# A fused four-stage kernel on one core: the setup ahead of the first softmax in another order

## The chip, the core and the metric

The kernel runs on one core of a Trainium2 chip. The metric is the device time of one execution in microseconds; the median of several executions counts. The data are float32 throughout, apart from the mask and a bfloat16 identity that is used to add it.

## What is computed

An input `x` of 16 items, 256 tokens by 256 features each, goes through four stages.

```python
# 0: adapter with an expert chosen per item, then a layer norm
h = gelu(x @ down_W.T + down_b) @ expert_W[id].T + expert_b[id] + domain_emb[id]
x = layernorm(h @ up_W.T + up_b + x) * gamma + beta
# 1: attention, scaled and shifted by an embedding of a timestep, then a feed-forward part
x = layernorm(x) * (1 + scale) + shift
s = q @ k.T / 4 + attention_bias          # 16 heads of 16; masked keys are -inf
x = x + softmax(s) @ v @ Wo + bo
x = x + gelu2(layernorm(x)*g2+beta2 @ W1 + b1) @ W2 + b2
# 2: one of three small networks, chosen per item, then a layer norm
# 3: finite differences of x on a 256 x 256 grid, one time step, max(., 0)
```

The attention bias alone is 16 x 16 x 256 x 256 floats (64 MB); it is read once, in pieces of four heads.

## The kernel before, in words

The items pass through the kernel as a stream. Nine generators each hold the work of one stage for all items: `adapt` (the adapter, two items at a time, called a pair), `prepare` (both norms ahead of the attention), `project` (q, k and v), `weigh` (scores and exponentials, four heads at a time), `attend` (transposing the weights and multiplying by v), `divide`, `enter` and `feed` (the rest of stage 1), `end` (stage 2) and `step` (stage 3). A planner, `Flow`, runs when the program is built. It keeps an estimated clock for each engine, which every generator advances with its costs (`flow.pe(1.0)`, `flow.dve(0.7, at)`), takes the generator that is due first among those that can start, and so fixes the order of the instructions on each engine. A `yield` gives the planner the choice: with a number it says when the next piece can start, with a function it says on what it depends (such as `("adapt", b) in done`). On the chip each engine then works through its own instructions in the order that the planner wrote down, and waits at each for its inputs.

What the change touches lies in the first 80 us. In the order of the program:

- Loads. SyncE asks for the tokens, `xt0` (the turned inputs of pair 0), the two expert matrices `e_w` of pair 0 (L303), `x0` (L251), the mask of item 0 (L378), the attention bias `side0` (L317), `x1`, `side1`, `Wo`, `side2`. ScalarE's queue asks for `w_down`, `cols`, `up`, `e_rows`, `w_ada` (L260), `rows_a` (L367) and `w_qkv` (L369), ahead of its first activation. All DMAs asked for by SyncE and ScalarE share eight semaphores, in turn; a DMA waits until the last one on its semaphore has landed.
- `idle` (L215) multiplies zeros; a count of 512 is one such matmul of 512 columns. It computes nothing that is used. Three run first (L226), one of 256 columns ahead of `p_u` (L570), and two ahead of pair 1 (L601).
- `adapt`, pair p: `p_h` (L543), a Gelu on ScalarE into `h1` (L547), `p_e` with the expert matrices (L558), `h2` on VectorE (L560; the trace calls `h1` and `h2` both `a_h`), `p_u` (L574), and the addition to each item's `x` on VectorE (L580). Beforehand `biased` (L527) has added the bias row `up_b` to `x` on GpSimd (L529). For pair 0 there are also `expert_bias`, `spread_mask(0)` (L382: the mask byte times a large negative number), `timestep` (Sin, Tanh, and the product `silu` on VectorE, L363), and `biased` for items 0 and 1.
- `prepare`, item b: statistics (L417 and L418 on VectorE, four small operations on GpSimd, L421 to L425: `rs` is one over the deviation), the first norm with gain and shift (L447 and L450 on VectorE for item 0; L456 and L457 on GpSimd for others), statistics again, and the second norm into `c_ln` (L433 or L438). For item 0 it also runs `condition` (`ps_a`, L500: 16-column matmuls that make scale and shift of all items) and, for item 1, `choose` (L970: 13 small operations on VectorE).
- `project`, item b: transposes `c_ln` (`c_t`, L464), scales it on ScalarE (`c_xt`, L632), multiplies by the three parts of `w_qkv` (`c_q` and `c_k` L646, `c_v` L689), and writes `c_qz` (L661 on VectorE, L665 on ScalarE), `c_kt` (L677) and `c_va` (L698).
- `weigh`, four heads m of item b: for item 0 it first adds the mask in the matmul (L733), then come the scores `c_s` (L738), and per head the bias and the row minimum on VectorE (L756) and the exponential on ScalarE (L767). For later items the mask is added to the bias by a DMA that GpSimd issues (L517).
- `attend` transposes the weights (`c_pt`), copies them out on VectorE (L472) or ScalarE (L474) and multiplies them by v (`c_c`, L821).

The Gelu, the Sin and the exponential need different function tables on ScalarE; the trace shows each change of table as an ACT_TABLE_LOAD.

Of the kernel before, what the change touches and what calls it, by code (L numbers as in the profile page):

```python
# [19 lines left out]
P = 128  # L20
B, S, D = 16, 256, 256
NC = S // P
# [148 lines left out]
def chain_kernel(ctx: ExitStack, tc: tile.TileContext, t: dict, out: bass.AP):  # L171
    nc = tc.nc
# [7 lines left out]
    def fixed(name, shape, dtype=F32, pool=const):  # L180
        return pool.tile(shape, dtype, name=name, tag=name)

    def load(name, src, shape, dtype=F32, engine=None, pool=const):
        got = fixed(name, shape, dtype, pool)
        (engine or nc.scalar).dma_start(out=got, in_=src)
        return got
# [4 lines left out]
    def chunked(w):  # L191
        return w.rearrange("(k p) n -> p k n", p=P)
# [3 lines left out]
    def misc(name, shape):  # L196
        numbers[name] = n = flow.take()
        return pp.tile(shape, F32, name=name, tag=f"m{n}")

    def free(name, at):  # L200

        flow.free_at[numbers.pop(name)] = at
        return at
# [11 lines left out]
    def idle(*columns):  # L215

        zeros = vas[1].rearrange("p c h e d -> p (c h e d)")
        name = f"idle{len(idles)}"
        idles.append(name)
        ps = misc(name, [P, NC * S])  # L220
        for n in columns:
            nc.tensor.matmul(ps[:, :n], zeros[:, :P], zeros[:, P : P + n], start=True, stop=True)
        free(name, flow.clock["PE"])
# [9 lines left out]
    def columns(name):  # L233
        return cols[:, COLUMN[name][0] : COLUMN[name][1]]
# [6 lines left out]
    def load_turned(p):  # L241

        arrives["t", p] = flow.clock["PE"] + 9.0 if p else 0.0
        xts[p] = xp.tile([P, 2, NC, S], F32, name=f"xt{p}", tag="xt", bufs=1)
        for i in range(2):
            nc.sync.dma_start(out=xts[p][:, i], in_=chunked(t["x_t"][2 * p + i]))

    def load_x(b):
        arrives["x", b] = flow.clock["PE"] + 7.0 if b > 1 else 0.0
        xs[b] = xp.tile([P, NC, D], F32, name=f"x{b}", tag="x", bufs=3)  # L250
        nc.sync.dma_start(out=xs[b], in_=chunked(t["x"][b]))  # L251
# [44 lines left out]
    e_ws = {}  # L296

    def load_expert(p):

        e_ws[p] = xp.tile([2 * A, A], F32, name=f"e_w{p}", tag="e_w")  # L300
        for i in range(2):
            e = nc.sync.value_load(e_idx[0:1, 2 * p + i : 2 * p + i + 1], min_val=0, max_val=E + 1)
            nc.sync.dma_start(  # L303
                out=e_ws[p][i * A : (i + 1) * A, :],
                in_=t["expert_W"][bass.ds(e, 1)].rearrange("e a o -> a (e o)"),
            )
# [51 lines left out]
    def timestep():  # L358
        for i, red in enumerate((sine, cosine)):
            nc.scalar.activation(emb[:, i, :], red, AF.Sin)  # L360
        nc.scalar.activation(th, emb, AF.Tanh, scale=0.5)
        nc.vector.tensor_scalar(emb, emb, 0.5, None, ALU.mult)
        nc.vector.scalar_tensor_tensor(silu, th, 1.0, emb, ALU.add, ALU.mult)  # L363
        flow.dve(0.25, flow.act(3.4))
# [1 line left out]

    rows_a = load("rows_a", rows(t["rows_a"]), [P, 5 * D])  # L367
    ln0_g, ln0_b, bv, bo, up_b = (rows_a[:, i * D : (i + 1) * D] for i in range(5))
    w_qkv = load("w_qkv", chunked(t["W_qkv"]), [P, NC, 3 * D])  # L369
    wq, wk, wv = (w_qkv[:, :, i * D : (i + 1) * D] for i in range(3))  # L370
    bqz = fixed("bqz", [P, NC])
    nc.vector.tensor_scalar(bqz, bq, columns("odd"), None, ALU.mult)
# [7 lines left out]
    def spread_mask(b):  # L380
        negs[b] = wp.tile([P, NC, S], BF16, name=f"neg{b}", tag="neg", bufs=2)
        nc.gpsimd.tensor_scalar(negs[b], m8s.pop(b), MASKED, None, ALU.mult)  # L382
        flow.pool(1.6)
# [96 lines left out]
    done = set()  # L480
    ready, ys, stats2, lns, hts, stats3 = {}, {}, {}, {}, {}, {}

    def expert_bias():

        ps_b = misc("ps_b", [2 * A, B // 2])
        for i in range(2):
            half = ps_b[i * A : (i + 1) * A, :]
            nc.tensor.matmul(half, e_rows[:, :A], e_hot[: E + 2, i::2], start=True, stop=False)
            nc.tensor.matmul(half, e_rows[:, A:], e_hot[: E + 2, i::2], start=False, stop=True)
        nc.vector.tensor_copy(e_add, ps_b)  # L490
        return free("ps_b", flow.dve(0.2, flow.pe(0.5)))
# [35 lines left out]
    def biased(b):  # L527
        x = xs[b]
        nc.gpsimd.tensor_tensor(x, x, up_b.unsqueeze(1).to_broadcast([P, NC, D]), ALU.add)  # L529
        flow.pool(1.35, arrives["x", b])  # L530
        done.add(("x", b))

    def adapt():

        for p in range(B // 2):
            yield lambda: p in e_ws
            yield arrives.get(("t", p), 0.0)
            parts = [slice(i * A, (i + 1) * A) for i in range(2)]
            w, xt = e_ws.pop(p), xts.pop(p)
            ps_h = misc(f"p_h{p}", [2 * A, S])  # L540
            for k in range(NC):
                for i in range(2):
                    nc.tensor.matmul(  # L543
                        ps_h[parts[i]], w_down[:, k, :], xt[:, i, k, :], start=k == 0, stop=k == NC - 1
                    )
            h1 = xp.tile([2 * A, S], F32, name=f"a_h1{p}", tag="a_h1", bufs=1)
            nc.scalar.activation(h1, ps_h, AF.Gelu, bias=columns("down_b"))  # L547
            at = free(f"p_h{p}", flow.act(0.47, flow.pe(1.0), "gelu"))
            if p == 0:
                expert_bias()  # L550
            yield at
            if p == 0:
                spread_mask(0)
                for b in range(2):
                    biased(b)
            ps_e = misc(f"p_e{p}", [2 * A, S])
            for i in range(2):
                nc.tensor.matmul(ps_e[parts[i]], w[parts[i]], h1[parts[i]], start=True, stop=True)  # L558
            h2 = xp.tile([2 * A, S], F32, name=f"a_h2{p}", tag="a_h2", bufs=1)
            nc.vector.tensor_scalar(h2, ps_e, e_add[:, p : p + 1], None, ALU.add)  # L560
            at = free(f"p_e{p}", flow.dve(0.4, flow.pe(0.5)))
            if p and 2 * p + 2 < B:
                load_turned(p + 1)
                load_expert(p + 1)
            if p:
                yield lambda: ("x", 2 * p + 1) in done
            yield at, 2
            if p == 0:
                timestep()
                idle(256)  # L570
            ps_u = [misc(f"p_u{2 * p + i}", [P, NC, D]) for i in range(2)]
            for c in range(NC):
                for i in range(2):
                    nc.tensor.matmul(  # L574
                        ps_u[i][:, c, :], h2[parts[i], c * P : (c + 1) * P], up[parts[i]], start=True, stop=True
                    )
            at = flow.pe(1.0)
            for b in (2 * p, 2 * p + 1):
                x = xs[b]
                nc.vector.tensor_tensor(x, ps_u[b % 2], x, ALU.add)  # L580
                adapted[b] = free(f"p_u{b}", flow.dve(0.7, at))
                done.add(("adapt", b))
                yield 0.0, 0

    def prepare():
        for b in range(B):
            yield lambda: ("adapt", b) in done
            x, at = xs.pop(b), adapted.pop(b)
            yield at, 0
            flow.spent += 0.75  # L590
            if b + 2 < B:
                load_x(b + 2)
                if b == 0:
                    load_turned(1)
                    load_expert(1)
            if b == 1:
                choose()
            stat, at = take_stats(f"0_{b}", x, at)
            if b == 0:
                condition()  # L600
                idle(512, 512)  # L601
            yield at, 0
            tmp = xp.tile([P, NC, D], F32, name=f"b_tmp{b}", tag="b_tmp", bufs=1)
            at = normalized_affine(x, x, stat, ln0_g, ln0_b, tmp, b == 0)
            yield at, 0
            stat, at = take_stats(f"1_{b}", x, at)
            if b == 0:
                conditioned()
                masked.update((m, 0.0) for m in range(4))
            yield at, 0  # L610
            if b > 1:
                yield lambda: ("turned", b - 2) in done
            ln = xp.tile([P, NC, D], F32, name=f"c_ln{b}", tag="c_ln", bufs=2)
            lns[b] = ln, normalized(ln, x, stat, b == 0)
            flow.spent += 1.5
            if b + 2 < B:
                biased(b + 2)
            done.add(("normal", b))

    def project():  # L620
# [622 lines left out]
```

## Time and profile before

| | us |
|---|---|
| median of three executions | 924.78 (921.94 to 926.36) |
| the profiled execution, its own time | 923.92 |
| its span, first to last instruction | 922.1 |
| TensorE matmuls busy | 882.4 (96%) |
| VectorE busy | 627.8 (68%) |
| ScalarE busy | 556.5 (60%) |
| GpSimd busy | 376.6 (41%) |
| mean granted TensorE clock | 0.978 |

The profile is of one execution. Its rows give for each instruction, or for a run of equal instructions, the start and the duration, and in brackets how long the engine had been idle before it and what ended that wait. PE is TensorE, PEld its weight loads, DVE is VectorE, ACT is ScalarE, POOL is GpSimd, SP is SyncE. A float32 matmul appears as two records. The granted clock is the share of full speed at which TensorE was allowed to run: a matmul of 256 columns takes about 380 ns at 1.00 and about 634 ns at 0.50 in this trace. The time of 922 us spans 40 slices on the page; TensorE's clock is 0.7 of full in the first of them, 0.6 in the second (both with rounding down to tenths) and 0.9 from the third to the last:

```profile
PE   7799898999999999999999999999999999999997
PEclk7699999999999999999999999999999999999999
DMA  9269978876777877778667776777667775850010
```

The DMA row is the busy share of the core's 16 DMA engines. They are full in the first slice, and again from about 65 to 112 us, when the large weights of the later stages are loaded beside the attention bias.

### The profile page before, as it was taken

Reading aid. Unit: us, or ns where it says so; the run is one execution under the profiler, and the core shown is the slowest. Engines: PE = TensorE matmul, PEld = TensorE weight load, DVE = VectorE, ACT = ScalarE, POOL = GpSimd, SP = SyncE. Lnnn points to the kernel's source line nnn. Section 1 sums busy time; section 2 is a strip of 40 time slices with the busy share of each in tenths; the row PEclk is TensorE's granted clock in tenths of the full one; section 3 lists DMA queues with packets and bytes.
Section 4 is the critical chain, followed back from the end, with each engine's and each line's share of the span. In section 5 each row is a group of like instructions: output and inputs, shape, how many; then the busy total and the mean of one; then the engine's idle time right before and its main releaser. Section 6 shows DMA issues by size and latency. Waiting matters only on the chain. (4 is left out here: it accounts for less than half of the span.)

```text
span 922.1 us, 18224 instructions
## 1 busy us (share of the span) xinstructions
PE 882.4 (96%) x6180; PEld 692.1 (75%) x6180; DVE 627.8 (68%) x2078; ACT 556.5 (60%) x1561; POOL 376.6 (41%) x514
## 2 busy tenths in 40 slices
PE   7799898999999999999999999999999999999997
PEld 4467585778787787877787778877878778877785
DVE  4477766888576777766767666766777676766443
ACT  2376747766566666766675767666675655656320
POOL 2234526653522425344543636154452525222331
PEclk7699999999999999999999999999999999999999
DMA  9269978876777877778667776777667775850010
GB/s 296 72 218 296 288 190 211 223 186 175 182 195 189 218 178 188 202 182 213 161 181 210 192 184 178 188 187 193 155 183 180 181 200 143 220 135 29 13 41 23
DMA packets 130972, 163.25 MB, mean 177 GB/s; under 512 B 12713, under 2 KB 94779, under 8 KB 130875
## 3 DMA queue, kind: packets, MB, share of 16 engines
q1 hardware_dynamic: 97920, 96.92, 33.1%
q0 software_dynamic: 31680, 62.92, 33.0%
q10 hardware_dynamic: 1275, 2.19, 0.7%
q8 instruction: 52, 0.85, 0.4%
q14 instruction: 45, 0.37, 0.1%
HBM read 94.89 MB, written 4.19 MB: 107 GB/s over the span
## 5 line engine op out<-in xcount | busy, mean ns | idle before, releaser
L767 ACT ACTIVATE c_pr<-c_sc,c_mx 128x256 f32<-128x256 f32 x512 | 254.9, 500 | 165.8 <-DVE c_mx L756 164.7
L756 DVE CUSTOM_DVE_ANT_0 c_sc<-c_s,side 128x256 f32<-128x256 f32 x512 | 193.6, 418 | 34.7 <-PE c_s L738 18.0
L464 PE MATMUL c_pt<-ident,c_pr 128*128 128x128 f32 x1024 | 143.5, 278 | 6.7 <-DVE x L580 2.1
L464 PEld LDWEIGHTS c_pt<-ident,c_pr 128*128 128x128 f32 x1024 | 116.8, 142 | 34.2 <-issue 11.9
L472 DVE COPY c_pts<-c_pt 128x512 f32<-128x512 f32 x175 | 117.2, 685 | 26.8 <-PE c_pt L464 26.5
L922 PE MATMUL d_f<-d_ht,w 128*128 128x256 f32 x512 | 122.3, 382 | 0.4
L421 POOL TENSOR_SCALAR rs<-mv 128x2 f32<-128x2 f32 x64 | 14.2, 222 | 253.2 <-DVE mv L418 252.7
L952 PE MATMUL d_o<-w,d_z 128*128 128x256 f32 x512 | 115.9, 380 | 0.1
L517 POOL DMA_DIRECT2D side<-neg x60 | 80.7, 1345 | 59.5 <-DMA side<-in_side 20.8
L952 PEld LDWEIGHTS d_o<-w,d_z 128*128 128x128 f32 x512 | 94.9, 190 | 12.5 <-DVE c_mx L756 0.6
L922 PEld LDWEIGHTS d_f<-d_ht,w 128*128 128x128 f32 x512 | 92.8, 190 | 15.1 <-issue 2.5
L767 ACT ACTIVATION_READ_ACCUMULATOR c_pr<-c_sc,c_mx 128x1 f32 x512 | 96.3, 188 | 0.0
L738 PE MATMUL c_s<-c_kt,c_qz 32*128 32x256 f32 x1024 | 78.3, 401 | 4.2 <-DVE c_mx L756 3.8
L821 PE MATMUL c_c<-c_pts,c_va 128*32 128x256 f32 x1024 | 72.6, 385 | 2.5 <-ACT c_pts L474 1.8
L738 PEld LDWEIGHTS c_s<-c_kt,c_qz 32*128 32x128 f32 x1024 | 49.1, 184 | 25.2 <-issue 12.2
L474 ACT COPY c_pts<-c_pt 128x512 f32<-128x512 f32 x81 | 45.5, 575 | 21.1 <-PE c_pt L464 21.0
L941 ACT ACTIVATE d_f<-d_z 128x512 f32<-128x512 f32 x64 | 38.4, 600 | 28.3 <-DVE d_z L938 27.2
L821 PEld LDWEIGHTS c_c<-c_pts,c_va 128*32 128x32 f32 x1024 | 27.9, 109 | 35.0 <-issue 18.2
L456 POOL TENSOR_TENSOR b_tmp<-b_tmp,rows_a 128x512 f32<-128x512 f32 x15 | 19.6, 1304 | 84.1 <-DVE b_tmp L433 65.7
L938 DVE TENSOR_SCALAR d_z<-d_f,cols 128x256 f32<-128x256 f32 x88 | 38.5, 479 | 17.3 <-PE d_f L922 17.2
L422 POOL TENSOR_TENSOR rs<-rs,inv_sqrt 128x2 f32<-128x2 f32 x64 | 46.0, 718 | 5.3
L960 DVE SCALAR_TENSOR_TENSOR y<-d_o,y 128x256 f32<-128x256 f32 x32 | 13.6, 424 | 45.4 <-PE d_o L952 45.4
(152 smaller groups left out, 1606.6 us busy)
## 6 DMA issues: line engine op xcount, KB each, us to landing
side<-in_side SPq DMA_DIRECT2D x256, 256.0 KB, 5.3
side<-neg POOLq DMA_DIRECT2D x60, 1024.0 KB, 8.1
d_w<-in_W_branch SPq DMA_DIRECT2D x16, 512.0 KB, 4.4
xt<-in_x_t SPq DMA_DIRECT2D x16, 256.0 KB, 5.2
x<-in_x SPq DMA_DIRECT2D x16, 256.0 KB, 5.9
out<-e_o SPq DMA_DIRECT2D x15, 256.0 KB, 3.9
w<-in_W SPq DMA_DIRECT2D x2, 1024.0 KB, 7.0
d_bout<-in_bl_branch SPq DMA_DIRECT2D x16, 128.0 KB, 4.3
```

Of the source, the lines that this page charges most:

```text
L422: nc.gpsimd.tensor_tensor(rs, rs, inv_sqrt, ALU.pow)
L464: nc.tensor.transpose(ps[:, k, c * P : (c + 1) * P], src[:, c, k * P : (k + 1) * P], ident)
L472: nc.vector.tensor_copy(dst, ps)
L474: nc.scalar.copy(dst, ps)
L517: nc.gpsimd.dma_start(out=sides[m].rearrange("p (h c) k -> p h (c k)", h=HB), in_=negs[m // 4].rearrange("p c k -> p (c k)").unsqueeze(1). ...
L738: nc.tensor.matmul(ps[i][:, c, :], qz[rows32, par, half, c * P : (c + 1) * P], k_t[rows32, half, :], start=b > 0, stop=b > 0 or c == NC - 1,)
L756: nc.vector.tensor_tensor_reduce(out=sc[:, c, :], in0=ps[i][:, c, :], in1=sb[:, i * NC + c, :], scale=-1.0, scalar=3.0e38, op0=ALU.add, op ...
L767: nc.scalar.activation(pr[:, c, :], sc[:, c, :], AF.Exp, bias=mx[:, c : c + 1], scale=-1.0, accum_out=sums[:, c, h : h + 1],)
L821: nc.tensor.matmul(ps_c[32 * i : 32 * i + 32, :], va[:, k, 4 * half + i, 2 * par : 2 * par + 2, :].rearrange("p e d -> p (e d)"), turned[i ...
L922: nc.tensor.matmul(ps_f[:, i, :], w1[:, k, f * P : (f + 1) * P], h_t[:, k, :], start=k == 0, stop=k == NC - 1,)
L938: nc.vector.tensor_scalar(z[:, i, :], ps_f[:, i, :], b1[:, f : f + 1], None, ALU.add)
L952: nc.tensor.matmul(ps_o, us[f // 2][:, f % 2, c * P : (c + 1) * P], w2[:, f, :], start=f == 0, stop=f == NF - 1,)
```

## The change

Five edits, all in the setup of the first items.

1. `W_qkv` is asked for on ScalarE's queue behind the first Gelu, instead of ahead of it.
2. In pair 0 the addition of `up_b` to item 0 is issued on GpSimd ahead of the spreading of item 0's mask, instead of behind it.
3. `up_b` is added to item 1 behind both norms of item 0 (together with that of item 2), instead of right after item 0's. Item 1's addition of the adapter's result on VectorE (L580 before, L582 after) waits in the plan until item 0 is normalised.
4. Pair 1 of the adapter can start only when item 1 has been normalised.
5. Four idle matmuls of 512 columns are issued behind `condition` instead of two.

```diff
-    w_qkv = load("w_qkv", chunked(t["W_qkv"]), [P, NC, 3 * D])
+    w_qkv = fixed("w_qkv", [P, NC, 3 * D])
...
         for p in range(B // 2):
-            yield lambda: p in e_ws
+            yield lambda: p in e_ws and (p == 0 or ("normal", 1) in done)
...
             if p == 0:
+                nc.scalar.dma_start(out=w_qkv, in_=chunked(t["W_qkv"]))
                 expert_bias()
             yield at
             if p == 0:
+                biased(0)
                 spread_mask(0)
-                for b in range(2):
-                    biased(b)
...
             for b in (2 * p, 2 * p + 1):
+                if b == 1:
+                    yield lambda: ("normal", 0) in done
                 x = xs[b]
                 nc.vector.tensor_tensor(x, ps_u[b % 2], x, ALU.add)
...
                 condition()
-                idle(512, 512)
+                idle(512, 512, 512, 512)
...
-            if b + 2 < B:
-                biased(b + 2)
+            for n in (1, 2) if b == 0 else (b + 2,) if b + 2 < B else ():
+                biased(n)
             done.add(("normal", b))
```

With these edits the planner writes another order for the first items, which can be read in the built program. On TensorE `p_h` of pair 1 now stands behind the first two transposes of item 0's weights, `p_e` behind item 1's `c_t`, and `p_u` of pair 1 ahead of item 1's q; `p_h` of pair 2 stands behind the third group of scores. On ScalarE the Gelu of pair 1 stands behind the first eight exponentials. On SyncE the loads `xt2` and `e_w2` stand behind `side3`, `W1` and `rows_b`, and `x4` behind `W2`. On GpSimd the spreading of item 1's mask and its first addition stand ahead of item 2's second statistics. Three copies of transposed weights go from ScalarE to VectorE. The number of matmuls differs only by the two idle ones, and from the places that the prediction names on, the orders are the same.

## The prediction

> **What bounds the kernel now.** I read four views. The page's busy shares come first: TensorE is busy 96% of the 922.1 us span, and the chain that ended last is followed back for only 2% of it, so neither says where time can be won. So I cut the span into stretches: TensorE is busy 648.9 of 660 us between 200 and 860 us, but only 34.4 of the first 44 us, before the first softmax. A microsecond won there moves the start of a stream that TensorE bounds. The order of instructions in the built program allows this reading: the orders of the two kernels differ only in the first 155 of TensorE's 2218 rows, and in the first 152, 47, 46 and 45 rows of VectorE, ScalarE, GpSimd and SyncE. From there on they are the same.
>
> The waits of TensorE, 0 to 50 us (total, times, longest):
> ```profile
> PE p_e L558 <- DMA e_w<-in_expert_W: 2.1, 1, 2.1
> PE p_h L543 <- DMA xt<-in_x_t: 1.5, 1, 1.5
> ```
> They name two transfers, but the timeline shows the real order (start, duration):
> ```profile
> 10.28 0.63 PE L558 MATMUL p_e<-a_h,e_w 64*64 64x256 f32 x2 [0.25 <-ACT a_h L547]
> ...
> 13.03 1.11 PE L558 MATMUL p_e<-a_h,e_w 64*64 64x256 f32 x2 [2.12 <-DMA e_w<-in_expert_W]
> ...
> 17.40 0.69 DVE L580 TENSOR_TENSOR x<-p_u,x 128x512 f32<-128x512 f32 x1 [2.42 <-PE p_u L574]
> ...
> 18.91 0.69 DVE L580 TENSOR_TENSOR x<-p_u,x 128x512 f32<-128x512 f32 x1 [0.82 <-POOL x L529]
> 19.52 0.42 DVE L417 BATCH_NORM_STATS2 st<-x 128x6 f32<-128x256 f32 x1
> ...
> 24.88 0.71 POOL L422 TENSOR_TENSOR rs<-rs,inv_sqrt 128x2 f32<-128x2 f32 x1
> ...
> 28.60 0.47 ACT L547 ACTIVATE a_h<-p_h,cols 128x256 f32<-128x256 f32 x1 [13.91 <-PE p_h L543]
> ...
> 30.32 0.48 DVE L560 TENSOR_SCALAR a_h<-p_e,e_add 128x256 f32<-128x256 f32 x1 [5.49 <-PE p_e L558]
> 30.72 0.73 DVE L433 TENSOR_SCALAR c_ln<-x,mv,rs 128x256 f32<-128x256 f32 x2
> 31.18 1.22 PE L464 MATMUL c_t<-ident,c_ln 128*128 128x128 f32 x4 [0.94 <-DVE c_ln L433]
> ```
> Three losses are seen. The second expert matrix holds p_e for 2.1 us. Item 0's statistics stand behind item 1's addition at 18.91. And c_ln (30.72) has its rs at 25.59, but stands on VectorE behind L560 of pair 1, which waits for pair 1's transfer, matmuls and Gelu.
>
> The clock, in two stretches (length, busy, granted clock, DMA share, GB/s):
> ```profile
> 15.00:24.00 9.00, 9.00 (x29) 0.50 1.08 340
> 33.10:39.20 6.10, 6.10 (x15) 0.50 0.19 54
> ```
> TensorE lost full clock in the 2.1 us wait (granted 0.98 at 11, 0.50 from 12) and did most of the q and k matmuls at half of it. Let T be the end of item 0's first scores: 43.51 now.
>
> **The change, part by part.**
>
> W_qkv later. Its 768 KB are issued at 7.01 now, after that behind the first Gelu, at about 10.3. The DMA engines are full from 4 to 24 us, at some 340 GB/s, so 768 KB are 2.2 us. Of two equal 16 KB e_w transfers, the one issued at 6.27 was there by 10.28; the other, issued near 7.7 behind W_qkv, took until 13.03 (the longest landing of e_w is 5.3 us). [...] The row has 5.3 us for 16 KB, and I take it: e_w near 10.9 (13.03 less 2.2). Then p_e ends near 11.5, h2 (L560) at 12.0, and p_u by 13.0 at full clock or 14.0 at half. ScalarE's queue is held by the issue (0.4 us); behind it stand Sin and Tanh with two table loads, so Tanh ends at 13.8 (13.4 now) and silu at 14.25, with L363 on VectorE directly ahead of item 0's addition. The addition thus moves from 17.40 to 14.3: -3.1. Bounds: 0 if e_w stays late, -3.1 if not. W_qkv itself, behind side0 and x0, should land by 18, before the q matmuls need it. Its issue waits on the semaphore of rows_a, landed near 10: nothing to 0.5 us. SyncE's next load (x1, 13.00) waits for e_w now, and moves up too.
>
> The order on GpSimd. up_b's addition to x0 stands behind the mask's spreading now (13.99 to 15.5, then to 16.84). Placed first it can end by 13 to 15.4, as x0 lands; the spread mask isn't read before the mask matmuls at 41. Nothing gained or lost by itself, but without it x0 would hold the 14.3.
>
> Item 1 behind the first norms. Statistics follow item 0's addition at once: 19.52 - 18.01 = -1.5. L560 of pair 1 leaves the place ahead of c_ln: 30.72 - 25.65 = -5.1. With the -3.1, c_ln starts near 21.0. The added wait: on VectorE x1's addition waits for GpSimd (21.6 to 22.9), and behind it stand 13 small operations (2.3 us), x1's statistics (1.2) and c_qz; all done by 27.1, while the q matmuls end near 27.4. Free, with 0.3 us to spare.
>
> Four idle matmuls for two. Two took 3.76 us in four pieces at half clock, 0.855 us apart; four are 6.8 us if the clock stays half. ps_a (3.6) starts with silu at 14.3 and ends at 17.9; so idle ends between 23.0 and 24.7, the earlier the sooner the clock rises. This now ends last, not c_ln (21.0, first half at 21.45): 2.4 us of the gain are lost here. That it does rise: the first idle block (three, 5.5 us, with the same 0.855 between pieces) was followed by p_h at 1.08 us, its time at full clock. I take c_t at 23.9, against 31.18: -7.3.
>
> Then c_t to T takes 12.3 us now, with q and k at half clock. At full clock item 1's q, k and v take 5.45 us from 53.95; chaining c_xt 24.75, q 25.35, c_qz 27.4, k_t to 30.35, v and mask to 31.7, scores: T = 32.9. That is -3.3 more, **-10.6** at T in all.
>
> After T the second pair comes back. It adds p_h (1.08) and p_e (0.65) to the stream, 1.7 us; its Gelu costs ScalarE two table loads. Trace: 1.28 + 0.47 + 1.28 = 3.0 us, next operation at once (53.92, 55.21, 55.70, 57.00), against an idle hole of 3.0 us before the exponential at 51.91: hidden. [...] But p_u now stands ahead of item 1's q, and three 0.685 us copies go from ScalarE to VectorE. Following both queues, c_s2 ends 1.1 us later than now relative to T, p_e of pair 2 waits for its Gelu, c_c for its copies, and c_t2 comes 3.2 us later, of which 0.5 is a transposition done earlier. On GpSimd the first mask addition goes ahead of rs of item 2 and waits for side4; I find it issued 0.7 us before rs is wanted. xt2 (0.5 MB) and x4 move into the stretch where the DMA engines are full (65 to 112 us), some 2.4 us; that lies beside the 2.7, not on top. I take **+2.7**, bounds 1.7 and 5.
>
> Sum: -10.6 + 2.7 = -7.9, from the profiled execution's 923.92 to 916.0. The median of the runs is 0.9 above that execution; I put the new median at **916.5**.
>
> **The rivals.**
> (B) e_w doesn't come earlier. [...] Then ps_a ends at 20.8, idle near 26.8, T = 35.8: -7.7 + 2.7, so 919 in that execution, 919.8 as median.
> (C) The clock falls back between idle and q. For: it fell in 8.6 to 12 us, TensorE 60% busy, and after 43.5 to 46.5, 51% busy; against: I count some 75% here. Q and k at half clock give 3.3 back: 920.
> (D) The full DMA stretch decides. GpSimd waited there 4.4 us for a side (at 99.07), VectorE then 3.0 for GpSimd, and TensorE 2.1 for VectorE. Two such waits more take 4 to 8 us: 920.5 to 924.5.
> (E) Slower: the mask additions, with side4 to side7 asked for behind xt2, e_w2 and w2 on SyncE's queue. If each of the four meets the 4.4 us wait in full, and nothing hides it, 17.6 take the place of 2.7: 923.9 - 10.6 + 17.6 = 931. It decides from 15 us of added waits on (10.6 + 4.6), and the four must all be on the path; of 4.4 us only 2.1 reached TensorE, which speaks against it.
> That the change doesn't do what it says I exclude: the built order shows each step.
>
> **How the numbers follow.** As forecast: 0.56, between 912.5 and 920 (idle's end and the 1.7 to 5 move it by 3, the run's clock phase and scatter of 922 to 926 by some more). B 0.13, C 0.12, D 0.12, E 0.07. Low end 911.5; the high end 922 takes in B, C and part of D. About 0.5% is what a measurement of this kernel can tell from no change: faster means below 920.2. That is nearly all of the forecast's case, two thirds of B and C and a little of D: 0.71; slower is E: 0.07; the rest 0.22.
>
> **What would show it.** p_e's second half without a wait near 11; item 0's statistics at 15; c_ln at 21, standing ready before c_t; idle ending at 23 to 25, and the granted clock 1.00 over q and k; T near 33; one Gelu between the exponentials in ScalarE's hole; c_t of item 2 some 31 us after T, where it is 27.9 now. The forecast is wrong if e_w still ends at 13, if W_qkv holds q, if the clock is 0.50 over q, or if the stretch from 65 to 112 us grows.

## The result and the profile after

The median goes from 920.99 us (919.32 to 926.36, 12 runs) to **916.39 us** (912.99 to 920.21, 12 runs); the ratio is 0.994 with an interval of 0.9916 to 0.9963. So the kernel is faster by 0.4 to 0.8%. The time lies 0.1 us from the forecast, but the gain is smaller than the forecast's: 4.6 us by the medians and 5.5 by the ratio, where the sum had 7.9 from the profiled execution and the forecast 8.3 from median to median (924.78 to 916.5). The median of before, with more runs, is 3.8 us below the 924.78 of its first three and 2.9 us below the execution that was profiled then.

The profiled execution after took 916.46 us, with a span of 914.7 and a mean granted clock of 0.984 (before: 923.92, 922.1, 0.978). The clock by slices of the page, of the kernel after:
```profile
PEclk9998998999999999999999999999999999999998
```
The 7 and the 6 of the first two slices are gone; an 8 has come in the fourth slice (69 to 91 us) and another in the seventh (137 to 160 us).

The waits of TensorE from 0 to 50 us, after (total, times, longest):
```profile
PE p_e L558 <- ACT a_h L547: 0.8, 2, 0.6
```
Neither transfer is named any more: p_e now waits only for its Gelu. The timeline after:
```profile
10.40 0.65 PE L558 MATMUL p_e<-a_h,e_w 64*64 64x256 f32 x4 [0.24 <-ACT a_h L547]
...
13.88 0.68 DVE L582 TENSOR_TENSOR x<-p_u,x 128x512 f32<-128x512 f32 x1
14.02 2.06 PE L500 MATMUL ps_a<-smalls,w_ada 128*128 128x16 f32 x16 [1.22 <-DVE smalls L363]
...
15.92 5.28 PE L222 MATMUL idle<-c_va 128*128 128x512 f32 x8
...
20.72 0.73 DVE L433 TENSOR_SCALAR c_ln<-x,mv,rs 128x256 f32<-128x256 f32 x2 [0.80 <-POOL rs L422]
...
21.18 0.87 PE L464 MATMUL c_t<-ident,c_ln 128*128 128x128 f32 x4
...
22.61 0.69 DVE L582 TENSOR_TENSOR x<-p_u,x 128x512 f32<-128x512 f32 x1 [1.16 <-POOL x L529]
...
22.71 2.02 PE L648 MATMUL c_q<-c_xt,w_qkv 128*128 128x256 f32 x8 [0.65 <-ACT c_xt L634]
...
29.04 1.15 PE L740 MATMUL c_s<-c_kt,c_qz 32*128 32x256 f32 x16
```
Item 0's addition comes at 13.88 where it came at 17.40, c_ln at 20.72 (30.72), c_t at 21.18 (31.18), and T, the end of item 0's first scores, is at 30.19 (43.5): 13.3 us earlier.

What became of the 13.3 us is read by matching TensorE's instructions of the two traces: the lengths of six stretches of the same stream. A group is four heads of one item; groups 0 to 3 are item 0's, 4 to 7 item 1's.

| stretch | before | after | change |
|---|---|---|---|
| start to T | 43.5 | 30.2 | -13.3 |
| T to item 2's c_t | 27.9 | 30.7 | +2.8 |
| to the scores of group 5 | 18.6 | 18.5 | -0.1 |
| group 5 to group 7 | 23.9 | 25.7 | +1.9 |
| group 7 to group 12 | 62.2 | 64.1 | +1.9 |
| group 12 to the end | 742.0 | 741.3 | -0.6 |

The changes are taken from the unrounded lengths; together they are -7.5. A little over half of what T gained is left. The place of the second loss, between groups 5 and 7, in the timeline after:
```profile
83.08 0.42 DVE L758 CUSTOM_DVE_ANT_0 c_sc<-c_s,side 128x256 f32<-128x256 f32 x1 [2.50 <-DMA side<-neg]
...
85.22 1.92 PE L823 MATMUL c_c<-c_pts,c_va 128*32 128x256 f32 x10 [4.29 <-ACT c_pts L474]
```
The mask additions of group 5, on GpSimd, before and then after:
```profile
76.40 1.36 POOL L517 DMA_DIRECT2D side<-neg  x1 [0.36 <-issue]
...
69.22 1.37 POOL L517 DMA_DIRECT2D side<-neg  x1 [4.81 <-issue]
```
TensorE's longest waits from 62 to 112 us, two of before and one of after:
```profile
PE c_pt L464 <- DVE x L580: 2.1, 1, 2.1
PE c_c L821 <- ACT c_pts L474: 1.8, 1, 1.8
...
PE c_c L823 <- ACT c_pts L474: 4.3, 1, 4.3
```
and in stretches of after, but for the row from 90 us, which is of before (length, TensorE, its loads, VectorE, ScalarE and GpSimd busy, granted clock, DMA share, GB/s):
```profile
15.70:19.10 3.40, 3.40 (x7) 1.71 (x7) 2.41 (x8) 0.00 (x0) 1.57 (x4) 0.51 1.10 355
...
22.70:26.30 3.60, 3.59 (x17) 3.08 (x18) 3.32 (x17) 0.41 (x1) 0.00 (x0) 1.00 1.10 349
...
84.00:90.80 6.80, 5.58 (x26) 3.31 (x26) 4.72 (x20) 4.89 (x18) 1.36 (x4) 0.50 1.10 360
...
90.00:113.90 23.90, 19.69 (x158) 13.15 (x150) 19.00 (x67) 16.60 (x47) 13.49 (x20) 1.00 1.00 300
...
79.40:105.10 25.70, 21.36 (x157) 14.44 (x150) 19.28 (x67) 16.66 (x47) 13.49 (x20) 0.87 0.99 292
```
The first two rows are the setup: half clock for 3.4 us only, and full clock over q. The others are the loss. The bias of group 5 (`side`), with the mask added to it by a DMA, is late: the addition is issued 7.2 us earlier than before, but takes 13.7 us to land where it took 8.3, and the scores need it 10.6 us earlier. VectorE waits 2.5 us for it, ScalarE behind VectorE reaches its copy of the transposed weights (c_pts) late, TensorE stands for 4.3 us, and the next 6.8 us run at half clock. Before, there were two smaller waits, of 1.8 and 2.1 us, and the clock stayed at 1.00. The last two rows set the way from group 5 to group 7 side by side: TensorE stands about as long in both (4.2 of 23.9 us and 4.3 of 25.7). The 1.9 us are half clock, behind one long wait in place of two short ones.

### The profile page after: what moved, and what is told of

The parts are those of the page before. It is cut to its first block, busy times and chain, and to the rows that moved or that the text cites. A ratio compares the mean times of both kernels' runs of the same rounds, so it can differ in the third digit from the quotient of the medians.

```text
span 914.7 us, 18234 instructions
## 1 busy us (share of the span) xinstructions
PE 877.9 (96%) x6184; PEld 689.3 (75%) x6184; DVE 630.1 (69%) x2081; ACT 555.3 (61%) x1558; POOL 377.2 (41%) x514
## 5 line engine op out<-in xcount | busy, mean ns | idle before, releaser
L464 PEld LDWEIGHTS c_pt<-ident,c_pr 128*128 128x128 f32 x1024 | 117.4, 143 | 32.5 <-issue 13.3
L472 DVE COPY c_pts<-c_pt 128x512 f32<-128x512 f32 x178 | 119.1, 684 | 27.1 <-PE c_pt L464 26.5
L421 POOL TENSOR_SCALAR rs<-mv 128x2 f32<-128x2 f32 x64 | 14.3, 223 | 252.2 <-DVE mv L418 251.4
L740 PEld LDWEIGHTS c_s<-c_kt,c_qz 32*128 32x128 f32 x1024 | 49.1, 184 | 25.7 <-issue 12.0
L474 ACT COPY c_pts<-c_pt 128x512 f32<-128x512 f32 x78 | 43.8, 575 | 21.3 <-PE c_pt L464 21.2
L940 DVE TENSOR_SCALAR d_z<-d_f,cols 128x256 f32<-128x256 f32 x88 | 38.4, 478 | 17.4 <-PE d_f L924 17.1
L422 POOL TENSOR_TENSOR rs<-rs,inv_sqrt 128x2 f32<-128x2 f32 x64 | 46.1, 720 | 5.3
```

The costliest lines, as they stand in the source:

```text
L422: nc.gpsimd.tensor_tensor(rs, rs, inv_sqrt, ALU.pow)
L464: nc.tensor.transpose(ps[:, k, c * P : (c + 1) * P], src[:, c, k * P : (k + 1) * P], ident)
L472: nc.vector.tensor_copy(dst, ps)
L474: nc.scalar.copy(dst, ps)
L740: nc.tensor.matmul(ps[i][:, c, :], qz[rows32, par, half, c * P : (c + 1) * P], k_t[rows32, half, :], start=b > 0, stop=b > 0 or c == NC - 1,)
L940: nc.vector.tensor_scalar(z[:, i, :], ps_f[:, i, :], b1[:, f : f + 1], None, ALU.add)
```

## The experiments

Every ratio is to the kernel before, with its 95% interval; T is that of the profiled execution.

| run | T us | median us | ratio |
|---|---|---|---|
| the change | 30.2 | 916.39 | 0.994 (0.9916 to 0.9963) |
| W_qkv later alone | 43.6 | 922.95 | 1.0021 (1.0002 to 1.0041) |
| change, W_qkv early | 34.1 | 920.74 | 1.0000 (0.9983 to 1.0016) |
| change, pair 1 early | 40.3 | 920.56 | 0.9993 (0.9967 to 1.0018) |
| change, two idle matmuls | 32.1 | 917.36 | 0.9957 (0.9939 to 0.9975) |
| change, mask spread first | 31.9 | 917.05 | 0.9947 (0.9927 to 0.9968) |
| change, grids later | 30.4 | 917.01 | 0.9957 (0.9932 to 0.9982) |
| before, grids later | 42.3 | 923.88 | 1.0008 (0.9986 to 1.0031) |
| before, four idle matmuls | 39.3 | 920.96 | 0.9988 (0.9964 to 1.0012) |
| change, mask by matmul, new plan | 31.9 | 934.15 | 1.0133 (1.0103 to 1.0163) |
| change, idle ahead of groups 6, 10 | 31.2 | 916.25 | 0.9935 (0.9909 to 0.9961) |
| change, idle ahead of groups 5, 10 | 30.3 | 914.79 | 0.9934 (0.9914 to 0.9954) |
| change, mask by matmul, same plan | 29.9 | 911.68 | 0.9908 (0.9882 to 0.9934) |

**One part alone, or one part undone.** First W_qkv alone, on the kernel before:
```diff
-    w_qkv = load("w_qkv", chunked(t["W_qkv"]), [P, NC, 3 * D])
+    w_qkv = fixed("w_qkv", [P, NC, 3 * D])
...
+                nc.scalar.dma_start(out=w_qkv, in_=chunked(t["W_qkv"]))
                 expert_bias()
```


> The kernel before with the first edit alone: W_qkv asked for behind the first Gelu. If W_qkv in the queue is what held the second expert matrix, p_e runs without a wait and ends near 11.2 (14.1 before), and item 0's statistics begin near 17.4 (19.5 before), held by the mask's spreading and item 1's addition. c_ln should still start near 30.7, since it stands behind pair 1, whose inputs land near 27: so T (end of the first scores) stays within 1 us of 43.5 and the time within 1.5 us of the kernel before. [...] If the early end of p_e is worth the gain by itself, the time is 3 us lower.

Its timeline:
```profile
9.78 0.71 PE L559 MATMUL p_e<-a_h,e_w 64*64 64x256 f32 x4 [0.47 <-DMA e_w<-in_expert_W]
...
32.10 0.48 DVE L561 TENSOR_SCALAR a_h<-p_e,e_add 128x256 f32<-128x256 f32 x1 [6.30 <-PE p_e L559]
32.50 0.73 DVE L433 TENSOR_SCALAR c_ln<-x,mv,rs 128x256 f32<-128x256 f32 x2
```
p_e is through at 10.5, and nothing comes of it: c_ln still stands on VectorE behind L561 of pair 1, now at 32.10, and T stays at 43.6. The time rises by 0.2%, a little more than was expected. Then the change with W_qkv asked for as early as before (the same diff turned round):

> The changed kernel with the first edit undone: W_qkv asked for ahead of the first Gelu. If W_qkv holds the second expert matrix, p_e ends at 14, item 0's addition is at 17.4 (13.9 in the changed kernel), the clock falls to half at 12, T is between 33 and 36 (30.2 in the changed kernel), and the time is 3 to 5.5 us above the changed kernel, close to the kernel before. If the order of the items is what counts, p_e's wait costs nothing that is not covered and the time is that of the changed kernel.

Its timeline:
```profile
12.89 0.64 PE L557 MATMUL p_e<-a_h,e_w 64*64 64x256 f32 x2 [2.57 <-DMA e_w<-in_expert_W]
...
16.30 3.59 PE L500 MATMUL ps_a<-smalls,w_ada 128*128 128x16 f32 x16
19.73 5.83 PE L222 MATMUL idle<-c_va 128*128 128x512 f32 x8
```
The second p_e waits 2.57 us, the clock is at half over ps_a (3.59 us instead of 2.06), and the idle matmuls end at 25.6, behind c_ln (23.31). The second e_w is issued at 7.7 us in this run, in both kernels and in the run before this one; it lands after 5.2 us here and 5.3 in the kernel before, and after 2.1 us in the two where W_qkv is asked for later. So the time lies between issue and landing, not in a later issue. T is 34.1, and the gain is gone, though T is still 9.4 us earlier than before. Then the change without the new condition for pair 1:
```diff
-            yield lambda: p in e_ws and (p == 0 or ("normal", 1) in done)
+            yield lambda: p in e_ws
```


> The changed kernel with the fourth edit undone: pair 1's p_h and p_e stand ahead of item 0's c_t again. If pair 1 is what held c_ln, c_t starts near 30 (21.2 in the changed kernel) and T is 39 to 42, while c_t of item 2 follows T by 28 us as in the kernel before and not by 30.7. The time is then 5 to 8 us above the changed kernel, so as the kernel before or slower by 1. If the return of pair 1 into the full stream costs what it gains, the time is that of the changed kernel.

Its timeline:
```profile
20.32 0.74 DVE L433 TENSOR_SCALAR c_ln<-x,mv,rs 128x256 f32<-128x256 f32 x2 [0.80 <-POOL rs L422]
...
27.40 2.62 PE L543 MATMUL p_h<-xt,w_down 128*64 128x256 f32 x8 [4.94 <-DMA xt<-in_x_t]
...
31.58 0.66 PE L464 MATMUL c_t<-ident,c_ln 128*128 128x128 f32 x4
```
c_ln is ready at 20.32, but pair 1 stands ahead of c_t on TensorE and waits there for its transfer: T is 40.3. From T to item 2's c_t it then takes 26.7 us instead of 30.7. So a late W_qkv and a late pair 1 are both needed. Item 1's addition behind the norms (edit 3) was neither run alone nor undone.

**The small parts.** Two idle matmuls instead of four (`idle(512, 512)`):

> The changed kernel with two idle matmuls of 512 columns instead of four. The idle work ends near 19.3 (21.2), c_t starts at 21.2 as before. If the idle work is what keeps the clock, the granted clock is 0.50 over the q and k matmuls and T is 3.3 us later (33.5); the time is 2 to 3.5 us above the changed kernel. If the clock holds without it, T stays at 30.2 and the time is the same.

The mask spread ahead of the addition to item 0 (`spread_mask(0)` ahead of `biased(0)`):

> The changed kernel with the second edit undone: item 0's mask is spread ahead of the addition of up_b to item 0. The mask lands near 12.7, so the spreading ends at 14.2 and x0's addition on GpSimd at 15.5 (12.7 in the changed kernel). If that comes last, item 0's addition on VectorE starts at 15.5 (13.9), c_ln at 22.3 (20.7) and T is 1.6 us later; the time is 1 to 2 us above the changed kernel. If silu holds the addition anyway, nothing moves.

T comes 1.9 and 1.7 us later in these two. With two idle matmuls 10.2 us of the setup run at half clock and c_q takes 3.78 us instead of 2.02; with the mask first item 0's addition comes at 14.51. Both medians are less above the change's (1.0 and 0.7 us) than was expected, and can't be told from it.

**The loss behind 80 us: the grids?** Stage 3's grids (1.8 MB) are asked for in the full stretch. They were moved four groups later, in the change and in the kernel before:
```diff
-        4: [later("grids", chunked(t["grids"]), [P, NC, 7 * S])],
+        8: [later("grids", chunked(t["grids"]), [P, NC, 7 * S])],
...
```


> The changed kernel with the 1.8 MB of grids asked for behind the ninth group of scores instead of the fifth; they are not read before the last stage of item 0, near 200 us. The changed kernel is 13.3 us ahead at T, 10.6 at item 2's c_t, and 8.7 at 130 us: the last 1.9 are lost between 80 and 105 us, where VectorE waits 2.5 us for a mask addition and TensorE then 4.3 us. If full DMA engines are the cause, that wait shrinks below 1 us, the clock does not fall at 84 us, and the time is 2 to 4 us below the changed kernel. If the wait is for the order of the queues and not for bytes, it stays and so does the time.

> The kernel before with the same later load of the grids. It has waits of 1.8, 2.1 and 0.3 us in the stretch from 93 to 106 us. If bytes are the cause, the time is 2 to 3.5 us below the kernel before, and the difference to the changed kernel with later grids is again 6 to 8 us: the two gains add. If the changed setup only moves its gain into this stretch, the difference between the two is the 10.6 us seen at item 2's c_t.

In the change VectorE's wait for the side falls from 2.5 to 1.3 us, TensorE's from 4.3 to 3.1, and the way from group 5 to group 7 from 25.7 to 24.7, but the time doesn't move. The grids are at most a part of the loss.

**The clock alone?** The kernel before with four idle matmuls (`idle(512, 512, 512, 512)`), and nothing else:

> The kernel before with one size changed: four idle matmuls in place of two behind the first statistics (item 0), and nothing of the new order. Theory A, the order theory: the start of item 0's first projection is set by c_ln of item 0 (30.72 us in the profile of before), which no idle matmul touches; the four idles end near 26, ahead of it, so only the projection's clock can change, T goes from 43.5 to 40 to 43 and the time by at most 1 us: 920 to 921.5, ratio 0.999 to 1.0005. Theory B, the clock theory: most of what the change gained is that TensorE was kept busy through its setup and so ran at full clock in it; then the four idles alone take 7 to 14 us of half clock out of the 27.3 us of the setup, and the time falls by 2 to 4 us, to 917 to 919, ratio 0.9955 to 0.998.

T is 39.3: 4.2 us earlier than in the trace of before, with 13.7 us at half clock in the setup instead of 27.3. But the profiled execution (914.54) is the lowest of twelve, and the ratio is 0.9988 with an interval on both sides of 1. Its single runs, taken together, had 27 us at half clock where the runs of before beside them had 34, and a mean of 920.1 against 921.7. So keeping TensorE busy gives at most a part of the gain.

**The mask additions?** Item 1's mask is added by matmuls, as item 0's is, so that the four DMAs which add it to groups 4 to 7 are gone:
```diff
-                masked.update((m, 0.0) for m in range(4))
+                masked.update((m, 0.0) for m in range(8))
...
-            if b == 0:
+            if b <= 1:
                 for i in range(4):
                     for c in range(NC):
-                        nc.tensor.matmul(ps[i][:, c, :], ident_b, negs[0][:, c, :], start=c == 0, stop=False)
+                        nc.tensor.matmul(ps[i][:, c, :], ident_b, negs[b][:, c, :], start=c == 0, stop=False)
...
-                        start=b > 0,
-                        stop=b > 0 or c == NC - 1,
+                        start=b > 1,
+                        stop=b > 1 or c == NC - 1,
...
+                if i == 0 and m == 1:
+                    spread_mask(1)
```


> The changed kernel with item 1's mask brought into its scores by matmuls, as item 0's is, in place of the four additions that DMAs make to its sides (issued at 57.0, 69.2, 75.8 and 91.0 us). Theory A: the 2.7 us at 60 us and the 1.9 us between the scores of groups 5 and 7 come of the mask additions in the stretch that is full of DMA; without them VectorE's wait of 2.5 us for an added side and TensorE's wait of 4.3 us at 81 us go, and the half clock of 6.8 us at 84 us with them. The added mask matmuls cost 4 groups of 1.0 us, so the time is 915 to 917, and the stretch from group 5's to group 7's scores is 22 to 24 us in place of 25.7, less the 2 us that the new matmuls add in it. Theory B: VectorE waits there for the plain loads of the sides as well, and the wait stays; then the time is 918 to 921.

18 us slower than the change: outside what either theory allows. The edit takes away times on which the planner works, and it wrote another plan for the whole stream (212 copies of transposed weights stand on VectorE, for instance, where the change has 178). The run says something of the plan and nothing of the mask; why that plan is slower was not followed. The last run does it with the plan kept.

**Idle matmuls in the stalls.** Four of 512 columns ahead of the scores of two groups, written into the scores' own buffer:
```diff
+            if m in (6, 10):
+                zeros = vas[1].rearrange("p c h e d -> p (c h e d)")
+                for _ in range(4):
+                    nc.tensor.matmul(
+                        ps[0].rearrange("p c k -> p (c k)"), zeros[:, :P], zeros[:, P : P + 512], start=True, stop=True
+                    )
+                flow.pe(0.0)
```


> The changed kernel with four more idle matmuls (512 columns each, 2.6 us together) ahead of the scores of group 6 (78.6 us) and of group 10 (137.9 us). Both stand ahead of a stall of TensorE, of 4.3 us at 80.9 and of 3.1 us at 138.6, in which VectorE doesn't take up the scores for 3 to 4 us anyway; each stall is followed by 6.8 us at half clock. Theory A, the clock theory: what was lost behind 80 us is clock, at about 0.3 us for each us at half clock; the idles fill 2.6 us of each stall, the clock stays up, the half clock of the profile falls from 30 to 17 to 24 us, and the time falls by 2 to 4 us to 912.5 to 914.5. Theory B: the stalls themselves are the loss, and the idles come on top where the stall is shorter in other executions: 916 to 918.

The expectation had the wrong group: the scores at 78.6 us are group 5's. Ahead of group 6 no stall was to be filled, and four idle matmuls take 3.6 us at full clock, not 2.6. At group 10 it did as expected: from group 9 to 12 the way is 33.6 us instead of 36.9, and no half clock follows. So with groups 5 and 10 (`if m in (5, 10)`):

> As the run with idle matmuls ahead of groups 6 and 10, but at the right place: the scores at 78.6 us are group 5's (group 6's come at 93.0, where TensorE has no stall, and there the idles cost 2.6 us). Four idle matmuls (2.6 us) ahead of the scores of group 5 and four ahead of group 10; nothing else differs from the changed kernel. Theory A, the loss behind 80 us is clock: around group 10 the idles took 3.3 us out of the way from group 9's to group 12's scores in that run; around group 5 the way to group 7 goes from 25.7 us to that of the kernel before, 23.9. Together 4 to 5 us: 911 to 913.5, and no half clock at 84 and 142 us. Theory B, the stall at 81 us is shorter in other executions than in the profiled one, and idles there come on top: 913.5 to 916.5.

Timeline and one stretch of that run:
```profile
78.36 3.60 PE L735 MATMUL c_s<-c_va 128*128 128x512 f32 x8
...
85.20 1.05 PE L830 MATMUL c_c<-c_pts,c_va 128*32 128x256 f32 x10 [1.01 <-ACT c_pts L474]
```
```profile
84.00:90.80 6.80, 5.79 (x52) 3.76 (x53) 6.10 (x22) 6.45 (x22) 1.52 (x5) 1.00 1.10 361
```
c_c goes on at 85.20 as it did at 85.22, since its input is no earlier, but at full clock, and is through in 1.05 us instead of 1.92. The profiled span is 909.7 us. That execution is again the lowest of its thirteen, and 2.5 of its 5.0 us against the change's lie behind group 12, where nothing was altered: it has no half clock there. The median, 914.79, stands to its own runs of before as the change does (0.9934 against 0.994), in the range of theory B. Over the runs the half clock falls from 23 to 13.5 us, and no gain can be told from it. (It is worked out as twice one less the mean clock, times the time: in the traces of before and after every stretch has a clock of 1.00 or 0.50.) The clock theory of the loss isn't shown by time; only the place of the half clock is.

**The mask additions, with the plan kept.** As above, but the planner still counts the additions; only the DMA is left out:
```diff
-        nc.gpsimd.dma_start(
+        if m > 7:
+            nc.gpsimd.dma_start(
...
-            if b == 0:
+            if b <= 1:
...
+                if b == 0:
                     flow.pe(1.0)
```


> As the run with item 1's mask by matmul, which let the planner order the whole kernel anew and so says nothing of the mask; here the planner's times are left as they were, and every engine but TensorE (32 more matmuls) and GpSimd (four additions fewer) keeps its order. Theory A, the mask additions cause the stall of 4.3 us and the clock behind it: the stall goes to under 1.5 us, no half clock stands at 84 us, and the way from group 5's to group 7's scores is 22 to 24 us without the 2 us of the new matmuls; these cost 4 us in all, so 914 to 918. Theory B, the sides' own loads are as late: the stall stays over 3 us and the time is 918 to 921.

Its timeline and one stretch:
```profile
80.19 1.04 PE L736 MATMUL c_s<-neg,ident_b 128*128 128x256 bf16 x8
81.16 1.15 PE L742 MATMUL c_s<-c_kt,c_qz 32*128 32x256 f32 x16
...
82.32 0.42 DVE L760 CUSTOM_DVE_ANT_0 c_sc<-c_s,side 128x256 f32<-128x256 f32 x1
...
84.46 1.05 PE L825 MATMUL c_c<-c_pts,c_va 128*32 128x256 f32 x10 [1.01 <-ACT c_pts L474]
```
```profile
84.00:90.80 6.80, 6.34 (x54) 4.22 (x58) 6.28 (x21) 6.45 (x18) 3.97 (x7) 1.00 0.77 286
```
VectorE takes up group 5 as soon as the scores are there, with no wait for a side; TensorE's stall is 1.0 us instead of 4.3; the clock stays at 1.00. From group 5 to group 7 the way is 21.2 us instead of 25.7, though two groups of mask matmuls (2.1 us) lie in it. That isn't one lucky trace: the other eight profiles of the changed kernel and its variants with the mask added by DMA have 3.4 to 6.8 us of half clock between these groups, this one none. Its median, 911.68, is the lowest of the study, below the expected 914 to 918. Against the change the ratio is 0.9908 / 0.994 = 0.9968, with a half-width of 0.0035 from the two intervals: a gain of about 3 us, just short of certain. Against the kernel before, 0.9% faster, it is.

**Order or clock?** The mean granted clock of every execution is known, so the single runs can be compared. The change's twelve had 23 us at half clock, the 131 runs of before in these comparisons 35; the means are 916.2 and 921.4. Within the kernel before, a run is longer by about 0.34 us for each us at half clock. By that the 12 us go with some 4 of the 5.2 us, and about 1 is left at equal clock. This is an estimate from runs that happened to differ, and it doesn't make the clock the cause: W_qkv early has the order and before's half clock (33 us), and before's time; pair 1 early, and the kernel before with four idle matmuls, have 27 us, and no gain clear of noise (0.5 and 1.6 us by the means). In these runs neither less half clock nor the new order brought a gain that could be measured without the other.

## Why the prediction was right, step by step

That the median came within 0.1 us is luck. The base was 3.8 us too high and the gain 3.7 too large. What was right is the path up to T, with one term too long; what followed T was priced too low.

**The base.** The new time was made from the profiled execution, 923.92, "0.9 above" for the median. That median rested on three runs. Over twelve it is 920.99, 2.9 below the profiled execution, while the kernel after has its profiled execution at its median; by this the gain of the medians is 2.9 us below that of the two profiled executions. The profiled execution of before had 27.3 us of half clock in its setup; the kernel before with later grids, whose work is the same up to there, had 17.1, T at 42.3 and item 2's c_t at 68.7 instead of 71.4.

**W_qkv.** Right, and the row of 5.3 us for 16 KB was the one to take. p_e ends at 11.05 (predicted 11.5), the addition is at 13.88 (14.3). The second e_w lands 2.1 us after its issue where it took 5.3: 3.2 us less, where the estimate from the 340 GB/s of the trace had 2.2. With everything else as in the change, asking for W_qkv early ends p_e at 13.5: 2.5 us, and by time 0.6%. Rival B's claim falls. Its price (T = 35.8, a gain of 5 us) was near in T (34.1), too low in time: that run gained nothing.

**GpSimd's order.** "Without it x0 would hold the 14.3": with the mask first the addition is at 14.51, and the time doesn't show it. Right in direction, and worth nothing that the time shows.

**Item 1 behind the norms.** Right in the trace: statistics at 14.60, c_ln at 20.72 (predicted 21.0). x1's addition waited 1.16 us for GpSimd at 22.61, and q was not held up.

**The idle matmuls.** This step failed. ps_a was to run at half clock until 17.9 and idle to end last, between 23.0 and 24.7, c_t at 23.9. ps_a took 2.06 us at full clock, with no wait of p_e ahead of it (3.59 us at half before, behind a wait of 2.1); only 3.4 us were at half clock, idle ended at 21.20, level with c_ln's first half, and c_t came at 21.18. These 2.7 us are the whole error of T; four more profiles with the same setup have T from 29.9 to 31.2. From c_t to T it was 9.0 us, as predicted, with full clock over q.

**After T.** c_t of item 2 came at T + 30.7, predicted "some 31", 2.8 us later than before relative to T (predicted +2.7). The tenth is luck: the profile of before has 3.4 us of half clock in this stretch, and four others with pair 1 ahead of T take 26.5 to 26.7 us for it instead of 27.9, against 29.3 to 31.7 where pair 1 comes behind T. The Gelu of pair 1, with two table loads, in ScalarE's timeline after:
```profile
37.35 1.28 ACT L547 ACT_TABLE_LOAD   x1
38.64 0.47 ACT L547 ACTIVATE a_h<-p_h,cols 128x256 f32<-128x256 f32 x1
39.13 1.28 ACT L769 ACT_TABLE_LOAD   x1
```
That is 3.1 us from the first load to the next exponential at 40.43, as in the rows of before (53.92 to 57.00).

**The full stretch.** "That lies beside the 2.7, not on top": wrong, it lay on top. Rival D had the place, and a chain close to it (a late side holds GpSimd, then VectorE, then TensorE), but 4 to 8 us for it; in the profile it is 1.9, and VectorE waits for the mask addition itself. The mask additions of E did reach the path, once, not four times. That they are the cause of this stall is shown by the last run, where without them the stall and the half clock are gone. Moving the grids took only 1 us off the stretch.

**Group 7 to 12.** Another 1.9 us that the sum didn't have: a stall of 3.1 us at 138.6 us, which both kernels have, is followed by 6.8 us of half clock instead of 3.4. TensorE stands 4.1 and 4.2 us in all, so these 1.9 us, like those between groups 5 and 7, are clock. Idle matmuls ahead of group 10 take the half clock away in the trace.

So two errors met: T was too pessimistic by 2.7 us, and what follows it too optimistic by 3.2. From one profiled execution to the other the sum is 0.4 us off (-7.9 against -7.5), with one execution of each. Still open is how much of the median's gain is order and how much clock: no run here held one fixed and moved the other.

## What to carry to other kernels

When a start is moved forward, look for the first place behind it where a transfer sets the pace, here a mask added by DMA, which was issued 7.2 us earlier and took 13.7 us to land instead of 8.3: a part of the gain was lost there, and taking that transfer away gave about 3 us more, just short of certain. Don't take an earlier start for a gain: with W_qkv early T came 9.4 us earlier and the time stayed. Take a median of a dozen runs as the base, not one profiled execution, before pricing a change of a few us. And an edit to a planned kernel can change the plan; an experiment has to keep the plan, or it measures that.

## What was not expected of the hardware

- Half clock came in these stretches: in the profile of before 27.3 us (from 11.95 us) and four times 3.4 us (from 46.1, 151.9, 838.0 and 909.7 us); in that after twice 3.4 us (from 15.7 and 32.8 us), three times 6.8 us (from 84.0, 142.0 and 899.8 us), and the last 1.2 us. In the kernel after a stall of 4.3 us was followed by 6.8 us at half clock; with the mask by matmul and the same plan, one of 1.0 us in the same place by none.
- The time of one kernel's executions goes with its half clock. Over 67 runs of the kernel before, a run was longer by 0.34 us for each us at half clock (mean 35 us). Part of this scatter lies behind group 12, in work that nothing here touched: with idle matmuls ahead of groups 5 and 10 the profile took 738.8 us there, without half clock, and those of before and after took 742.0 us, with 6.8 us of it, and 741.3 us, with 8.0. But where these idle matmuls took some 10 us of half clock out (23 to 13.5 us over the runs), the time didn't follow (0.994 and 0.9934 of before).
- A 16 KB transfer took 5.3 us to land (before) and 5.2 (the change with W_qkv early) when 768 KB of another queue were asked for ahead of it, and 2.1 us (the change, and W_qkv later alone) where they were asked for behind it; TensorE waited 2.1 and 2.57 us for it in the first two, and not at all and 0.47 us in the others.
- As many matmul records (6216) under another plan (another order, and 212 copies of transposed weights on VectorE instead of 178) took 934.15 us instead of 911.68.
